# One long spectral piece to a tick in place of two, and the second run of gates four ticks later

## The chip, the cores and the metric

The kernel runs on one core of a Trainium2 chip. The metric is the device time of one execution in microseconds (us). Before the change the median of three runs is 10126.7 us (10123.93 to 10132.92).

## The reference: what is computed

The input `x` is 8 elements of 8 channels of 512 x 512 numbers in fp32. Two layers follow each other, and both add their result to their input.

```python
x = x + _L0_conv_ref(_gn(x), ...)   # spectral layer
x = x + _L1_conv_ref(_gn(x), ...)   # cellular automata and a gate
```

Layer 0 normalises in groups, takes every second row and column, keeps 8 x 4 modes of the two-dimensional Fourier transform, mixes the channels of each mode with complex weights, and evaluates the result at all 512 x 512 points. Layer 1 normalises the sum again. It runs 15 steps of a coupled map, with a hidden network and a gate beside it:

```python
for _ in range(STEPS):
    mapped = R * grid * (1.0 - grid)
    local = _conv(mapped, K_local, groups=C_OUT)
    physics = (1.0 - EPS) * mapped + EPS * local
    grid = (1.0 - BETA) * physics + BETA * drive
cml_out = jnp.clip(grid, 0.0001, 1.0 - 0.0001)
h = jax.nn.relu(_conv(x, Wp, bp))
nca_out = jax.nn.sigmoid(_conv(h, Wu, bu))
gin = jnp.concatenate([x, cml_out, nca_out], axis=1)
g = jax.nn.sigmoid(_conv(jax.nn.relu(_conv(gin, Wg1, bg1)), Wg2, bg2))
return g * cml_out + (1.0 - g) * nca_out
```

## The kernel before

The program is written out in full, in one order per engine, which `keep_order` fixes: every engine executes its instructions in the order of the source. There is no loop on the device. Dependences between engines are semaphores, and all loads and stores of the main part are issued by SyncE (SP) in order.

The eight elements go through a pipeline. While element b runs the coupled map and the hidden network, the gates of element b-1 are computed and the spectral layer of element b+1. Time is planned in ticks, 75 (`TICKS`) to an element. One call of `work` emits one tick:

- Two convolutions of the coupled map (`convolve`, L523), one per set of 128 partitions; 192 matmul records of L528 in a tick. The map's channels are two halves of four, each half five sets and fifteen steps. `settle` (L577) adds the drive `dE` or `dO` on VectorE (L583) and squares on ScalarE (L589); at step 13 `dO` is shifted on GpSimd (L593). `renew` (L535) exchanges the edges of the sets by small DMAs.
- None, one or two rounds of the hidden network (`Hidden.round`, L620): 24 matmul records each (L628), evicted half by ScalarE (L634) and half by VectorE (L636). After each second round, `Hidden.point` (L643) multiplies `h` by `w_u` (L647).
- Other work, handed out by `Others`. `Others.first` comes between the rounds and `Hidden.point` and gets two pairs of PSUM banks; `Others.second` comes after it and gets one. `first` takes a gate's 3 x 3 convolution (`Gate.conv`, L693) if one was loaded in an earlier tick, and then `second` takes its pointwise part (`Gate.point`, L710). Without a gate both take pieces of the spectral layer.

The spectral layer of an element, `layer0` (L318), is a generator cut into pieces by `yield`. Before each piece stands what it needs (`need`): a channel number means that this channel must have been fetched in an earlier tick; `LATER` (-2) that the piece may only be the first of its call; `LONG` (-1) or a channel number makes it a long piece; nothing means that it may come at any time. In order the pieces are: eight transforms, one per channel (four bn_stats on VectorE, L332; matmuls L336); the statistics (`group_stats`, L299, matmuls L303 and L311); the mixing of modes (L361 to L391); and then for each channel the first half of the synthesis (L430, an addition L433 and two bn_stats L435), the rows of the next channel (`over_rows`, L395, matmuls L398, evicted by ScalarE L402), and the second half, with the statistics and the normalising (L414) of each pair of channels in between. `Element.spectral` (L771) refuses a long piece when the tick has already had two, counted in `Others.longs`.

`Others.feed` (L793) runs at the start of a tick. It loads gates, up to two waiting at a time, in ticks from `GATES[0]` on and before `GATES[1]`, and again from `GATES[2]` on; an element has 43. A gate's load is six DMAs, three into `gin` and three into `mix`, in slots of a pool of five (`shared`) that the fetched channels of `x` use too. From tick 26 (`SPECTRAL_FROM`) on it fetches up to two channels of `x` per tick, 1 MB each and sixteen in all, when a slot is free. After `feed`, `Half.prepare` (L495) loads `dE` and `dO` of the next half into 15 slots (`sets`) as they come free; for the next element this begins in tick 70. It also emits the scaling of `dO` (L521) on GpSimd and the first square (L508) on ScalarE.

On GpSimd a gate has a subtraction (L703) and a product (L721); VectorE closes it with L726 in the next tick, between the two settlings, and SP stores it (L733).

As the code orders it, a middle element (1 to 6) has in ticks 3 to 27 the first 25 gates, in 28 to 45 the spectral pieces, in 46 to 51 nothing besides the map and the hidden network, in 52 to 69 the other 18 gates, and in 70 to 74 nothing again. Element 0 has no gates, and its spectral pieces stand in ticks 0 to 18. Element 7 has gates and no spectral pieces. After it a tail computes the last element's hidden rounds and gates.

Of the kernel before, what the change touches and what calls it, by code (L numbers as in the profile page):

```python
# [52 lines left out]
GR = 12  # L53
TICKS = STEPS * 5
ROUNDS, ROUNDS_LAST, FIRST_ROUNDS = 128, 48, 8
GATES, SPECTRAL_FROM = (2, 27, 51), 26
SLAB, HALO, SETS = 32, 3, 5
SHARED = 5
LONG, LATER = -1, -2
# [67 lines left out]
def conv_layers(ctx: ExitStack, tc: tile.TileContext, a, out):  # L127
# [614 lines left out]
    class Element:  # L742
# [28 lines left out]
        def spectral(self, ps, n, longs):  # L771

            need = self.need
            if not self.pieces or need == LATER and n or need is not None and need >= LONG and longs > 1:
                return False
            if need is not None and need >= 0 and now[0] <= self.at.get(need, now[0]):
                return False
            self.bank.append(ps)
            self.need = next(self.pieces, self)
            self.bank.clear()  # L780
            if self.need is self:
                self.pieces, self.need = None, None
            return True
# [216 lines left out]
```

## Time and profile before

| | us |
|---|---|
| median of the runs | 10126.7 |
| profiled execution, its own time | 10129.58 |
| its span | 10127.8 |
| VectorE busy | 5848.6 |
| ScalarE busy | 4299.5 |
| GpSimd busy | 1766.8 |
| mean granted clock of TensorE (share) | 0.983 |

The profile is that of one execution. Lines are those of the kernel; busy is the time in which an engine had an instruction running; an arrow in a row points to what ended a wait. "issue" stands for time in which an engine waited for nothing that the profile shows. TensorE's weight loads (PEld) overlap its matmuls. The granted clock is the share of full speed that TensorE's throttle allowed; a DMA share is the mean busy share of the 16 DMA engines.

### The profile page before, as it was taken

The page shows a single profiled execution, that of the slowest core. Times are in us where ns is not written, and L with a number is a line of the kernel's source. Part 1 is how long each engine was busy: PE and PEld are TensorE (multiplying, and loading weights), DVE is VectorE, ACT ScalarE, POOL GpSimd, SP SyncE. Part 2 cuts the span into 40 slices and gives each one's busy share as a digit, 9 for nine tenths or more (in the row PEclk, how much of TensorE's full clock was granted, in tenths as well). Part 3 has the DMA queues.
Part 4 walks back from the last instruction along what each step waited for, and adds up shares of the span by engine and source line. Part 5 has one row for each costly group of instructions (what it writes and reads, how often), then busy time and mean ns, then how long its engine had stood idle before and what let it go on. Part 6 is the DMA issues. An engine that isn't in the chain of part 4 may idle for free. (4 is left out here: it accounts for less than half of the span.)

```text
span 10127.8 us, 353307 instructions
## 1 busy us (share of the span) xinstructions
PE 9436.5 (93%) x160496; PEld 4308.9 (43%) x160496; DVE 5848.6 (58%) x6067; ACT 4299.5 (42%) x4445; POOL 1766.8 (17%) x1406
## 2 busy tenths in 40 slices
PE   6998999999999999999999999999999999998999
PEld 3444444444444444444444444444444444444333
DVE  5654555755557555665555655566555665555555
ACT  2444444444444444444444444444444444444433
POOL 2010111202112021111211112111121201312212
PEclk9999999999999999999999999999999999999999
DMA  5231255535555465544555455554555535663578
GB/s 170 81 84 48 62 147 137 152 103 141 142 149 147 109 150 135 153 138 121 142 137 147 127 123 144 138 141 129 134 146 134 157 117 132 155 145 95 139 194 199
DMA packets 625565, 1353.50 MB, mean 134 GB/s; under 512 B 73067, under 2 KB 73195, under 8 KB 594051
## 3 DMA queue, kind: packets, MB, share of 16 engines
q1 hardware_dynamic: 621728, 1329.77, 50.7%
q8 instruction: 1261, 20.66, 0.9%
q14 instruction: 238, 1.94, 0.1%
q10 hardware_dynamic: 2338, 1.13, 0.0%
HBM read 992.27 MB, written 268.78 MB: 125 GB/s over the span
## 5 line engine op out<-in xcount | busy, mean ns | idle before, releaser
L528 PE MATMUL pair<-m,band 32*32 32x512 f32 x115200 | 4118.2, 608 | 177.2 <-issue 109.1
L589 ACT ACTIVATE m<-m 128x1024 f32<-128x1024 f32 x2240 | 2360.0, 1055 | 2811.5 <-DVE m L583 2695.1
L528 PEld LDWEIGHTS pair<-m,band 32*32 32x32 f32 x115200 | 2268.6, 104 | 1943.4 <-issue 1106.4
L628 PE MATMUL pair<-cols,w_p 32*128 32x511 f32 (+1 forms) x24576 | 2874.7, 605 | 42.8 <-issue 22.2
L583 DVE SCALAR_TENSOR_TENSOR m<-pair,dO 128x1024 f32<-128x1024 f32 x1280 | 1507.5, 1219 | 1372.5 <-PE pair L528 1176.3
L583 DVE SCALAR_TENSOR_TENSOR m<-pair,dE 128x1024 f32<-128x1024 f32 x1120 | 1319.7, 1220 | 1222.4 <-PE pair L528 1039.2
L628 PEld LDWEIGHTS pair<-cols,w_p 32*128 32x128 f32 x24576 | 1284.6, 187 | 1647.0 <-issue 1138.0
L636 DVE TENSOR_SCALAR h<-pair,b_p 128x1024 f32<-128x1024 f32 x1024 | 1313.5, 1283 | 838.7 <-PE pair L628 838.2
L634 ACT ACTIVATE h<-pair,b_p 128x1024 f32<-128x1024 f32 x1024 | 1140.7, 1114 | 990.0 <-PE pair L628 981.7
L721 POOL TENSOR_TENSOR mix<-mix 96x512 f32<-96x512 f32 x344 | 437.5, 1272 | 4413.2 <-ACT mix L719 4067.7
L647 PE MATMUL pair<-h,w_u 128*32 128x512 f32 x8192 | 1014.9, 606 | 205.4 <-DVE h L636 189.3
L698 PE MATMUL pair<-gin,w_g 128*32 128x511 f32 (+1 forms) x8256 | 965.7, 599 | 5.9 <-DMA mix<-xn 3.3
L703 POOL TENSOR_TENSOR mix<-mix 96x512 f32<-96x512 f32 x344 | 437.9, 1273 | 1420.7 <-DMA mix<-nca 1340.7
L593 POOL TENSOR_SCALAR dO<-dO 128x2048 f32<-128x2048 f32 x80 | 431.7, 5408 | 1263.2 <-DVE m L583 1263.1
L647 PEld LDWEIGHTS pair<-h,w_u 128*32 128x32 f32 x8192 | 254.3, 110 | 848.8 <-issue 367.6
L660 ACT ACTIVATE y<-y,b_u 128x512 f32<-128x512 f32 x256 | 184.8, 722 | 908.4 <-DVE y L656 908.4
L698 PEld LDWEIGHTS pair<-gin,w_g 128*32 128x32 f32 x8256 | 237.2, 110 | 681.6 <-issue 464.8
L715 PE MATMUL pair<-mix,w_g 128*32 128x512 f32 x2064 | 358.8, 595 | 85.2 <-DVE mix L708 85.2
L654 ACT COPY y<-pair 128x512 f32<-128x512 f32 x256 | 149.9, 585 | 631.1 <-PE pair L647 527.0
L708 DVE TENSOR_SCALAR mix<-pair,b_g 128x512 f32<-128x512 f32 x344 | 257.9, 750 | 254.2 <-PE pair L698 254.2
L726 DVE SCALAR_TENSOR_TENSOR mix<-mix,back 96x512 f32<-96x512 f32 x344 | 316.1, 919 | 150.8 <-POOL mix L721 150.8
L521 POOL TENSOR_SCALAR dO<-dO,base 128x512 f32<-128x512 f32 x320 | 226.8, 724 | 783.0 <-DMA dO<-xn 728.0
(85 smaller groups left out, 2642.2 us busy)
## 6 DMA issues: line engine op xcount, KB each, us to landing
gin<-xn SPq DMA_DIRECT2D x344, 384.0 KB
cols<-xn SPq DMA_DIRECT2D x256, 512.0 KB
x<-in_x SPq DMA_DIRECT2D x120, 1024.0 KB
gin<-cml SPq DMA_DIRECT2D x344, 320.0 KB
gin<-nca SPq DMA_DIRECT2D x344, 320.0 KB
dE<-xn SPq DMA_DIRECT2D x320, 256.0 KB
dO<-xn SPq DMA_DIRECT2D x320, 256.0 KB
mix<-xn SPq DMA_DIRECT2D x344, 192.0 KB
```

What stands on the lines that cost most here:

```text
L528: nc.tensor.matmul(ps[h // 2][32 * t : 32 * t + 32, h % 2], band[at, c0 + (t if step % 2 else h), dx], m[at, t, dx : dx + N], start=(n == ...
L583: nc.vector.scalar_tensor_tensor(u[:, at], ps[q], FLOOR, d[:, at], ALU.max, ALU.add)
L589: nc.scalar.square(u[:, at], u[:, at])
L593: nc.gpsimd.tensor_scalar(d, d, 0.5, None, ALU.add)
L628: nc.tensor.matmul(ps[g // 2][:, g % 2, lo:hi], w_p[p, dx, i % 2], self.cols[p, i // 2, at : at + hi - lo], start=(n == 0), stop=(n == 2), ...
L634: nc.scalar.activation(h[:, :2], ps[0], AF.Relu, bias=b_p)
L636: nc.vector.tensor_scalar(h[:, 2:], ps[1], b_p, 0.0, ALU.add, ALU.max)
L647: nc.tensor.matmul(ps[32 * g : 32 * g + 32], w_u[:, r % 4], h[:, g], start=(r == self.hs[0][0]), stop=(r == self.hs[-1][0]), tile_position ...
L698: nc.tensor.matmul(ps[32 * j : 32 * j + 32, lo:hi], gband[:, dx], gin[:, j, at : at + hi - lo], start=(n == 0), stop=(n == 2), tile_positi ...
L703: nc.gpsimd.tensor_tensor(d, d, ng, ALU.subtract)
L715: nc.tensor.matmul(ps[at], gpoint[:, at], mix[:, 3], start=True, stop=True, tile_position=(0, 32 * j),)
L721: nc.gpsimd.tensor_tensor(d, d, mix[: GR * C, 2], ALU.mult)
```

## The change

Two numbers. In `Element.spectral`, a long piece is refused when the tick has had one long piece already, in place of two. `GATES[2]`, the tick from which an element's second run of gates is loaded, is 55 in place of 51.

```diff
@@ -53,7 +53,7 @@
 GR = 12
 TICKS = STEPS * 5
 ROUNDS, ROUNDS_LAST, FIRST_ROUNDS = 128, 48, 8
-GATES, SPECTRAL_FROM = (2, 27, 51), 26
+GATES, SPECTRAL_FROM = (2, 27, 55), 26
 SLAB, HALO, SETS = 32, 3, 5
 SHARED = 5
 LONG, LATER = -1, -2
@@ -771,7 +771,7 @@
         def spectral(self, ps, n, longs):
 
             need = self.need
-            if not self.pieces or need == LATER and n or need is not None and need >= LONG and longs > 1:
+            if not self.pieces or need == LATER and n or need is not None and need >= LONG and longs:
                 return False
             if need is not None and need >= 0 and now[0] <= self.at.get(need, now[0]):
                 return False
```

With it the spectral pieces of a middle element stand in ticks 28 to 54, tick 55 has neither pieces nor gates, the 18 gates of the second run stand in 56 to 73, and tick 74 has nothing again. In element 0 the pieces stand in ticks 0 to 27. No instruction is added or removed, and the tail's order is the same.

## The prediction

> **What bounds the kernel now.** I read the page first. TensorE is busy 93% of the span, VectorE 58%, ScalarE 42%: TensorE is the bound, and what can be won is in its gaps.
>
> ```profile
> PE 9436.5 (93%) x160496; PEld 4308.9 (43%) x160496; DVE 5848.6 (58%) x6067; ACT 4299.5 (42%) x4445; POOL 1766.8 (17%) x1406
> q8 instruction: 1261, 20.66, 0.9%
> ```
>
> The table of waits, filtered to PE (total us, times, longest), names the gaps. The reader is to see three kinds: waiting for the hidden layer's eviction, waiting for statistics, and "issue", in which nothing in the trace is waited for.
>
> ```profile
> PE pair L647 <- DVE h L636: 189.3, 147, 1.6
> ...
> PE pair L528 <- issue: 109.1, 65, 4.5
> ...
> PE pair L303 <- DVE mv L294: 79.2, 26, 12.5
> ```
>
> Then the timeline of PE. A tick begins with 192 records of L528, so counting 192 of them divides the trace into 600 ticks, 75 for an element. Tick numbers below count from an element's start; means are over elements 1 to 6, whose plans are alike. First an empty tick (element 2, tick 50): 1.52 us pass before L647, since only then is h there.
>
> ```profile
> 3363.02 6.58 PE L528 MATMUL pair<-m,band 32*32 32x512 f32 x192
> 3369.53 5.43 PE L628 MATMUL pair<-cols,w_p 32*128 32x512 f32 x48
> 3376.48 1.92 PE L647 MATMUL pair<-h,w_u 128*32 128x512 f32 x16 [1.52 <-DVE h L636]
> ```
>
> Then tick 44, where two synthesis halves (both L430, a "long" piece each) stand in one tick and the statistics at once need them. The eight L430 take 1.04 us; VectorE's additions and bn_stats for both make PE wait 3.37 us.
>
> ```profile
> 3285.79 1.04 PE L430 MATMUL pair<-e,ty 8*128 8x512 f32 x8
> 3287.40 1.92 PE L647 MATMUL pair<-h,w_u 128*32 128x512 f32 x16 [0.57 <-DVE h L636]
> 3292.70 0.58 PE L303 MATMUL pair<-mv,avg 128*128 128x1 f32 x2 [3.37 <-DVE mv L294]
> ```
>
> Last the windows, one per tick (span, then busy time of PE, PEld, DVE, ACT, POOL, granted clock, DMA share, GB/s): ticks 35, 41, 50, 51, 52 and 70 to 74 of element 2. In the spectral ticks 35 and 41 the clock falls to 0.79 and 0.90; an empty tick is 15.31, a gate tick 17.21; 51, with two gate loads at once, 20.31; DMA is idle in 70, 0.72 busy in 71 and 72, full in 73 and 74.
>
> ```profile
> 3122.68:3140.48 17.80, 17.41 (x244) 7.62 (x245) 14.21 (x15) 1.51 (x2) 7.64 (x9) 0.79 1.03 243
> 3224.60:3240.73 16.13, 15.72 (x251) 7.10 (x249) 11.58 (x12) 6.40 (x7) 0.00 (x0) 0.90 0.60 210
> 3363.02:3378.33 15.31, 13.79 (x260) 6.67 (x256) 7.97 (x7) 7.07 (x7) 0.00 (x0) 1.00 0.33 78
> 3378.33:3398.64 20.31, 16.01 (x260) 6.79 (x256) 7.28 (x6) 6.93 (x7) 1.26 (x1) 0.92 0.65 155
> 3398.64:3415.85 17.21, 17.21 (x290) 7.73 (x286) 9.38 (x9) 7.65 (x8) 0.00 (x0) 1.00 0.41 111
> 3698.78:3714.09 15.31, 13.79 (x259) 6.70 (x256) 7.94 (x7) 7.03 (x7) 1.98 (x2) 1.00 0.16 51
> 3714.09:3729.41 15.32, 13.80 (x260) 6.66 (x257) 7.97 (x7) 7.06 (x7) 0.31 (x1) 1.00 0.72 166
> 3729.41:3744.73 15.32, 13.79 (x261) 6.65 (x257) 8.42 (x7) 4.93 (x5) 2.40 (x4) 1.00 0.72 172
> 3744.73:3761.16 16.43, 14.22 (x260) 6.36 (x257) 10.33 (x9) 2.95 (x3) 3.41 (x7) 1.00 0.96 239
> 3761.16:3776.75 15.59, 14.11 (x260) 7.15 (x256) 9.55 (x8) 6.61 (x5) 3.80 (x9) 1.00 0.97 256
> ```
>
> Over ticks 28 to 74 a middle element takes 777.2 us: 41.4 of waits, 10.4 of "issue", 35.3 at half clock. Waits and issue off, and half of the half-clock time, 707.8 remain as TensorE's work, which the change doesn't touch.
>
> [...] eight L430 take 1.04 us, four 1.03. [...] The page's q8 line is that (20.66 MB in 1261 packets, 16.4 KB each); not hidden here: I take "issue" to be PE waiting for such a block behind bursts of data.
>
> **The change, part by part.** No instruction is added; only the order differs. [...] Empty ticks outside 0 to 2 fall from 11 (46 to 51, 70 to 74) to two (55, 74). The number of hidden rounds in a tick (two, or one in pairs of ticks) keeps its place.
>
> *Spectral ticks.* A two-round tick holds 13.80 us of work and 1.52 of wait. A transform piece adds 0.96 (two make 15.71, no wait left, so (15.71 - 13.80)/2), a synthesis half 0.93 (the wait falls from 1.52 to 0.59 with one): alone each fits into the wait, and the tick stays at about 15.35.
> - 28 to 35, the eight transforms: 12.5 (one round) + 5 x 15.4 + 10.9 + 14.3 = 114.7. In 35 the wait for statistics stays in part: four bn_stats (2.4 us) fewer lie before it, but also one transform on PE; 1.4 in place of 3.3.
> - 36 to 38, means and mixing, as now: 17.6 + 15.5 + 17.6 = 50.7.
> - 39 to 52, synthesis: seven two-round ticks with one half each, 15.35 to 15.6, together 108.2; 43, 44 and 51 (over_rows with a half, 2.1 of work against 1.5 of wait, like today's 16.40 in tick 43) 16.8, 16.3, 16.4; one-round ticks 40, 41, 47, 48, estimated between an empty 10.7 or 11.9 and today's 14.5 to 17.3 with two halves: 12.8, 12.2, 15.0, 14.2. Together 211.9.
> - 53: as 44 now (19.18) less one addition and two bn_stats (1.20 + 1.29): 16.7. 54: 10.9.
> - Dips: from 27 us of half clock in ticks 28 to 45 I leave 12, a loss of 6. Bounds: 0 and 13.5, all of today's loss.
> - The fetches of x spread from ticks 27 to 33 over 27 to 36 and meet the loads of the second half (tick 35 is at 1.03): 3 for issue, between 0 and 6. On SP such a fetch waits for the slot's last bn_stats (L332; SP waits 68.2 us for it in all, 10 times); behind it stand dE loads that are issued two ticks ahead: nothing.
>
> Together 413.9 for 28 to 54, with 55 at 16.5: 11.9 empty plus 4.6, since today's tick 51 is 5.2 over empty in the mean for the same double load, and moves with it.
>
> *Gates.* 56 to 69 are gates before and after: 241.0. 70 to 73 turn from empty (61.9) into two-round gate ticks of 17.7, today's mean, 70.8. 74: 16.2.
>
> *What collides.* Gate loads now issue in ticks 70 to 72, each six DMAs of 1.6 MB ahead of the next element's dE and dO on SP's queue; the out store, waiting for L726 on SP, joins up to 74. A gate tick's DMA share is near 0.6, an empty one's 0.16, so a load is 0.45 x 17 = 7.6 us of all engines, three 23 us. The slack in 70 to 72 is (0.84 + 0.28 + 0.28) x 15.3 = 21 us, plus 6 from longer ticks. It just fits, in bursts of 3.6 MB in 71 and 72, larger than tick 51's 3.2. I take 8 us of issue and dips; the bounds are 1 and 23 (the rival below). On POOL, the dO scaling (L521, 2.7 us, waiting for its load) now stands ahead of L703 and L721 in 72 and 73. Behind L721 waits L726 on VectorE, ahead of the next settling. I put the load that it waits for 10 to 16 us later in 73 than now; with 2.7 + 1.3 + 1.3 L721 ends between 15 and 21 us after that tick's start, and L726 is due at 17.2 + 5: nothing, with 1 us of cover.
>
> Sum per middle element: 413.9 + 16.5 + 241.0 + 70.8 + 16.2 + 8 = 766.4, against 777.2: -10.8. The same by gaps: 707.8 + 29 of waits + 16 of issue + 8.5 of dips = 761.3, -15.9. I take -13, times six -78. Element 0 has no gates: 27 ticks (1 to 27) of 424.5 us hold 34.2 of waits and 47.8 at half clock; spread out I make them 403, -21. Element 7's gates only change places with empty ticks; the tail is the same: 0. Total -99. The profiled execution took 10129.58 for a span of 10127.8; the median is 10126.7, 3 us lower. 10126.7 - 99 gives 10028.
>
> **Rivals.**
> 1. *Dips go and the collision is harmless*: the sum without the allowances of 6, 3 and 8 is 749.4, with 1 for the collision 750.4, -26.8 per element, and -21 for element 0: 9945. For it: gate ticks elsewhere lose only 0.5 us to bursts, and 73 and 74, full of DMA, hardly any. [...]
> 2. *Dips stay as they are*[...]. 7.5 us more per element (13.5 in place of 6) leaves -5.5, with the collision at 12 in place of 8 it leaves -1.5; element 0 keeps half, -10: 10084 to 10108. I take 10100, where faster and no change meet. [...]
> 3. *Slower: the next element's loads come late.* In element 7, ticks 36 to 39, loads of a half meet short ticks; those four take 57.8 us where their likes take about 35, 23 lost.
>
> ```profile
> 9192.69 4.52 PE L528 MATMUL pair<-m,band 32*32 32x512 f32 x128 [3.29 <-issue]
> ...
> 9207.95 3.98 PE L628 MATMUL pair<-cols,w_p 32*128 32x512 f32 x17 [4.13 <-issue]
> ```
>
> The place is ticks 71 to 77: gate loads stand ahead of dE and dO in SP's order and on the DMA engines. It decides once the last dO lands over 9 us later than now: its scaling (L521) ends at 3795.2 in element 2, and the settling that adds it stands in tick 77, which begins at 3800.9 and convolves for 3 us first. Price: 23 at the boundary as in element 7, in place of the 8, and if the three gate loads stay almost wholly unhidden (20 late of 23) another 20 - 9 = 11 in the first ticks; 26 x 6 = 156 over the forecast: 10184. Against: 27 us of slack for 23 of loads.
>
> That the change doesn't do what it says can be excluded: the order of pieces follows from the code alone.
>
> **How the numbers follow.** Forecast 10028: 0.47. Rival 1: 0.20. Rival 2: 0.18, of it 0.08 within no change. Rival 3: 0.15. A measurement here tells 0.2%, 20 us, from none. Faster 0.77, same 0.08, slower 0.15. The range, 9930 to 10140, leaves out rival 3 and a quarter of rival 1.
>
> **What would show it.** L647's wait for h falls well below 189 us; L303's wait falls from 79 to about 50; tick 53 is near 16.7; the clock in the spectral ticks is above 0.95. Wrong, if issue grows by over 10 us per element in ticks 70 to 77, if L528 or L508 waits there for dE, or if the half-clock time stays at 338 us.

## The result, and the profile after

The change made the kernel slightly faster: median 10093.04 us of six runs (10081.33 to 10109.42) against 10125.32 us before (six runs), ratio 0.9973 with a 95% interval of 0.9961 to 0.9985. That is 32 us, a third of the 99 that were forecast. The profiled execution of the changed kernel is the fastest of its six, so the two profiles lie 48.7 us apart (spans 10079.1 and 10127.8), more than the medians. Where parts are added up below, they are parts of these 48.7.

The first lines are from the page of the changed kernel and from its table of waits, filtered to PE (total us, times, longest). The last line is L398's in the kernel before.

```profile
PE 9432.0 (94%) x160496; PEld 4303.4 (43%) x160496; DVE 5851.5 (58%) x6067; ACT 4294.7 (43%) x4445; POOL 1768.5 (18%) x1406
...
PE pair L647 <- DVE h L636: 130.5, 150, 1.6
PE pair L528 <- issue: 125.0, 73, 4.4
...
PE pair L528 <- ACT h L634: 50.5, 40, 11.5
PE pair L303 <- DVE mv L294: 47.3, 19, 12.4
PE pair L398 <- ACT h L634: 39.5, 27, 8.7
```

```profile
PE pair L398 <- ACT h L634: 10.5, 15, 0.9
```

The reader is to see two falls and two rises. The waits that the change aims at fell as forecast: L647's for `h` from 189.3 to 130.5 us, L303's for statistics from 79.2 to 47.3. But L398 now waits 39.5 us for ScalarE (before: 10.5, and never over 0.9), and L528's issue went from 109.1 to 125.0.

The timeline of PE shows that the pieces alone behave as worked out. Tick 53 of element 2 has one half of the synthesis before the statistics, and the wait, 3.37 us in tick 44 before, is now 0.93:

```profile
3368.90 1.02 PE L430 MATMUL pair<-e,ty 8*128 8x512 f32 x4
3370.50 1.92 PE L647 MATMUL pair<-h,w_u 128*32 128x512 f32 x16 [0.57 <-DVE h L636]
3373.36 0.38 PE L303 MATMUL pair<-mv,avg 128*128 128x1 f32 x2 [0.93 <-DVE mv L294]
```

The loss is in the windows of ticks 36 to 38 of element 2 (span, busy time of PE, PEld, DVE, ACT, POOL, granted clock, DMA share, GB/s), below with ticks 70 to 74. The last line is tick 38 of the same element in the kernel before, where synthesis pieces stand in it:

```profile
3074.05:3092.13 18.08, 17.01 (x323) 8.78 (x323) 12.38 (x23) 7.92 (x8) 4.90 (x6) 1.00 0.99 265
3092.13:3114.82 22.69, 17.40 (x259) 6.92 (x257) 10.39 (x12) 8.36 (x7) 7.93 (x11) 0.85 0.95 234
3114.82:3142.29 27.47, 20.19 (x276) 7.69 (x273) 12.52 (x18) 10.98 (x10) 10.83 (x10) 0.79 0.48 122
...
3643.01:3660.16 17.15, 17.15 (x289) 7.66 (x287) 10.04 (x10) 7.03 (x7) 3.23 (x3) 1.00 0.59 146
3660.16:3678.40 18.24, 18.24 (x289) 7.74 (x286) 9.34 (x9) 8.23 (x9) 2.51 (x2) 1.00 0.95 187
3678.40:3695.55 17.15, 17.15 (x290) 7.59 (x287) 12.12 (x11) 5.03 (x5) 5.70 (x6) 1.00 0.63 141
3695.55:3717.66 22.11, 19.66 (x289) 7.81 (x286) 12.54 (x11) 4.11 (x5) 5.22 (x6) 0.92 1.02 231
3717.66:3734.03 16.37, 14.89 (x260) 7.12 (x257) 10.38 (x9) 6.81 (x5) 5.11 (x9) 1.00 0.95 244
```

```profile
3176.51:3193.89 17.38, 17.38 (x274) 9.64 (x272) 13.47 (x14) 11.74 (x11) 10.84 (x10) 1.00 0.89 321
```

Tick 38 takes 27.47 us with TensorE's clock at 0.79. Of the gate ticks at the end, which I had feared, only 73 is much longer than a gate tick elsewhere (21.2 us in the mean of the six elements).

Split into ticks as in the prediction, a middle element (mean of 1 to 6, us) came out so:

| ticks | forecast | after |
|---|---|---|
| 28 to 35, transforms | 114.7 | 117.8 |
| 36 to 38, means and mixing | 50.7 | 66.2 |
| 39 to 52, synthesis | 211.9 | 213.6 |
| 53, 54 | 27.6 | 27.2 |
| allowances for dips and fetches, held in the rows above | 9 | |
| 55 | 16.5 | 13.2 |
| 56 to 69 | 241.0 | 240.2 |
| 70 to 74 | 95.0 | 91.2 |
| 28 to 74 | 766.4 | 769.4 |

Before, 28 to 74 took 777.2. Ticks 0 to 27 became 3.1 longer, so a middle element gains 4.8 (1241.7 to 1236.9), of a forecast of 13. Element 0 gained 26.4, element 7 lost 7.3.

What happens in tick 38 stands in four timelines of the changed kernel, of SP, GpSimd, ScalarE and PE in this order:

```profile
3115.14 0.38 SPq L611 DMA_DIRECT2D cols<-xn  x1
3117.77 0.79 SPq L391 DMA_DIRECT2D om<-of_sin  x1
3118.61 3.42 SPq L569 DMA_DIRECT2D cml<-m  x4
```

```profile
3127.99 0.11 POOL L507 MEMSET m<- 128x8 f32 x1 [17.20 <-DMA cml<-m]
```

```profile
3116.30 1.99 ACT L508 ACTIVATE m<-dE,mhalf 128x2048 f32<-128x2048 f32 x1
3128.14 2.00 ACT L508 ACTIVATE m<-dE,mhalf 128x2048 f32<-128x2048 f32 x1 [9.85 <-POOL m L507]
3130.04 2.93 ACT L589 ACTIVATE m<-m 128x1024 f32<-128x1024 f32 x3
3132.88 1.09 ACT L634 ACTIVATE h<-pair,b_p 128x1024 f32<-128x1024 f32 x1
```

```profile
3121.97 5.48 PE L628 MATMUL pair<-cols,w_p 32*128 32x512 f32 x48
3134.03 1.93 PE L398 MATMUL pair<-e,om 16*32 16x512 f32 x8 [6.57 <-ACT h L634]
```

Read from below: PE's L398 waits 6.57 us for ScalarE's L634. L634 stands in ScalarE's order behind L508, the square of the fifth set of the second half, which waits 9.85 us for GpSimd's memset L507. The memset waits for the slot that the last set of the first half leaves, that is for its store `cml<-m`. SP issued this store at 3118.61, behind `om<-of_sin`, the store of the mixing's result. L398 waits in this way in tick 38 of all six middle elements, 1.3 to 8.7 us each.

In the kernel before, the same store went out before its tick 38 began at 3176.51. The memset waited there for VectorE and not for the store, and ScalarE waited 1.19 us for it (SP, GpSimd and ScalarE):

```profile
3172.61 3.82 SPq L569 DMA_DIRECT2D cml<-m  x4
```

```profile
3181.68 0.11 POOL L507 MEMSET m<- 128x8 f32 x1 [12.18 <-DVE m L583]
```

```profile
3181.82 2.00 ACT L508 ACTIVATE m<-dE,mhalf 128x2048 f32<-128x2048 f32 x1 [1.19 <-POOL m L507]
```

The mixing lay in ticks 32 and 33, and `om<-of_sin` went out at 3108.32, just after tick 34 began. SP stood waiting for VectorE there too, and longer: 126.4 us in the whole kernel before, 67.4 in the changed one. But in element 2 the next `cml` store came 25 us behind it. What changed is not the wait, but what stands behind it.

### The profile page after: what moved, and what is told of

The parts are those of the page before. It is cut to its first block, busy times and chain, and to the rows that moved or that the text cites. A ratio compares the mean times of both kernels' runs of the same rounds, so it can differ in the third digit from the quotient of the medians.

```text
span 10079.1 us, 353020 instructions
## 1 busy us (share of the span) xinstructions
PE 9432.0 (94%) x160496; PEld 4303.4 (43%) x160496; DVE 5851.5 (58%) x6067; ACT 4294.7 (43%) x4445; POOL 1768.5 (18%) x1406
## 3 DMA queue, kind: packets, MB, share of 16 engines
q8 instruction: 1261, 20.66, 0.9%
## 5 line engine op out<-in xcount | busy, mean ns | idle before, releaser
L528 PE MATMUL pair<-m,band 32*32 32x512 f32 x115200 | 4107.0, 605 | 205.4 <-issue 125.0
L528 PEld LDWEIGHTS pair<-m,band 32*32 32x32 f32 x115200 | 2256.1, 103 | 1945.9 <-issue 1111.4
L634 ACT ACTIVATE h<-pair,b_p 128x1024 f32<-128x1024 f32 x1024 | 1140.3, 1114 | 995.7 <-PE pair L628 977.7
L647 PE MATMUL pair<-h,w_u 128*32 128x512 f32 x8192 | 1010.1, 604 | 153.0 <-DVE h L636 130.5
L647 PEld LDWEIGHTS pair<-h,w_u 128*32 128x32 f32 x8192 | 250.9, 110 | 787.1 <-issue 383.8
```

What stands on the lines that cost most here:

```text
L528: nc.tensor.matmul(ps[h // 2][32 * t : 32 * t + 32, h % 2], band[at, c0 + (t if step % 2 else h), dx], m[at, t, dx : dx + N], start=(n == ...
L634: nc.scalar.activation(h[:, :2], ps[0], AF.Relu, bias=b_p)
L647: nc.tensor.matmul(ps[32 * g : 32 * g + 32], w_u[:, r % 4], h[:, g], start=(r == self.hs[0][0]), stop=(r == self.hs[-1][0]), tile_position ...
```

## The experiments

Theory A: the early part of the spectral layer, one transform to a tick, ate the gain, since it moves fetches and mixing onto the half boundary in ticks 35 to 38. Its variants are A1, the fetches of `x` collide with the second half's loads; A2, the mixing's store stands before the cml store in SP's order; A3, the moved pieces keep the engines busy there. Theory B: the gates' shift ate it. Theory C: splitting the synthesis gains little. All ratios are against the kernel before on the same chip, with its 95% interval; before ran in 10127.46 us beside the first four runs and in 10125.95 beside the others.

**The gates alone** (`e1_gates_only`).

```diff
-GATES, SPECTRAL_FROM = (2, 27, 51), 26
+GATES, SPECTRAL_FROM = (2, 27, 55), 26
```

> Two long pieces to a tick as before, only the second run of gates four ticks later. Theory A (the early transforms, one to a tick, ate the gain; the gates' shift costs little): per middle element +12 for ticks 70 to 73, -10 for 52 to 55, +3 in the next element's first ticks, and +7 in element 7: +35 in all, 10145 to 10170 beside about 10125 before. Theory B (the gates' shift ate it): +70 or more, 10195 and up. If the shift costs nothing: 10125.

Measured: 10161.32 us, ratio 1.0036 (1.0021 to 1.005). That is about 34 us more: the shift costs what A puts on it, not what B needs. In its profile ticks 70 to 74 take 94.0 against 78.1, 51 to 55 take 68.6 against 83.4, and the next element's ticks 0 to 2 take 2.7 more. By itself the shift is a loss. It is the price of having ticks 51 to 54 for the spectral layer.

**The synthesis alone** (`e3_late_one_51`): two transforms to a tick as before, of the later long pieces one.

```diff
-need is not None and need >= LONG and longs > 1:
+need is not None and need >= LONG and longs > (0 <= need < C):
```

> Two transforms to a tick as before, one synthesis piece to a tick as in the change, gates at 51 as before (the pieces just fit, ticks 28 to 50). Theory A: ticks 34 to 50 fall from 274 to about 255 in each middle element, element 0 gains 15: -100 to -130, 9995 to 10025. Theory C (splitting the synthesis gains only what fills empty ticks, 5 to 8 us per element): -30 to -60, 10065 to 10095. Theory B expects the same as A here, since the gates stay.

Measured: 10066.83, ratio 0.9939 (0.9924 to 0.9954), a gain of 61, just above the upper end of C's range and well below A's. So one part of the change, without the gates' shift that it doesn't need, gives about twice the whole change. Ticks 34 to 50 take 269.3 us in its profile (273.9 before), where A expected 255. In them ticks 35 to 38 still take 72.5 us (73.9 before), with 4.8 of issue and 10.1 at half clock: the half boundary has stalls with synthesis pieces in it too.

**The transforms alone** (`e4_early_one`).

```diff
-need is not None and need >= LONG and longs > 1:
+need is not None and need >= LONG and longs > (not 0 <= need < C):
```

> One transform to a tick as in the change, two synthesis pieces as before, gates at 51. Theory A: ticks 28 to 38 cost 184 as in the changed kernel, later ones as before: +10 per middle element, -10 in element 0: +30 to +60, 10155 to 10185. Theory B: a gain of 5 to 10 per element from transforms that fit into the wait for h: -40 to -60, about 10075.

Measured: 10144.55, ratio 1.002 (1.0012 to 1.0029): slower, by less than A expected, and not the gain of B. Ticks 28 to 34 fall to 99.5 us from 115.4, and 35 to 38 rise to 83.8, tick 38 alone to 26.3, nearly the changed kernel's 84.3 and 26.4. The loss there, against the forecast, comes with the transforms' order and without the gates' shift. Against before, it is another place that makes this variant slower: ticks 28 to 38 together are 6.0 us shorter (183.3), and 39 to 54 are 10.4 longer (264.6), since the synthesis pieces that stood in 34 to 38 now follow there, two to a tick.

**Fetches held back** (`e5_hold_x`): of the sixteen fetches of `x`, the last seven wait until tick 38. It is the changed kernel with

```diff
-                if spectral and (t >= SPECTRAL_FROM or not e):
+                if spectral and (t >= SPECTRAL_FROM or not e) and (not e or after.fetched <= C or t >= 38):
```

> The changed kernel, but the second copies of x after the first wait until tick 38, so that four fetches leave ticks 33 to 36. Theory A1 (these fetches meet the loads of the second half): ticks 35 to 38 fall from 84 to 68 to 72, -70 to -100 against the changed kernel's 10093, 9995 to 10025. Theory A2 (not the bytes, but the pieces of the mixing and their stores in SP's order at the half boundary): within 15 of 10093. Theory B: within 15 of 10093.

Measured: 10089.03, ratio 0.996 (0.9945 to 0.9974), like the changed kernel. A1 as the only cause falls. Issue in tick 37 went from 2.5 to 0.1 us, but tick 38 stayed at 25.7. SP's timeline says why:

```profile
3108.39 0.38 SPq L611 DMA_DIRECT2D cols<-xn  x1
3114.65 0.79 SPq L391 DMA_DIRECT2D om<-of_sin  x1
3115.49 3.00 SPq L569 DMA_DIRECT2D cml<-m  x4
```

SP has issued all that stood ahead by now, and stands still from 3108.8 to 3114.65, until VectorE has finished the mixing. The store behind it goes out no earlier in the tick than in the changed kernel (3.8 us after its beginning).

**The store of om behind the cml store** (`e6_om_later`): `later(1, ...)` puts it at the end of its tick. It is the changed kernel with

```diff
-        nc.sync.dma_start(out=om[8:, :, :8], in_=of_sin)
+        later(1, lambda: nc.sync.dma_start(out=om[8:, :, :8], in_=of_sin))
```

> The changed kernel, but the store of of_sin into om is issued at the end of its tick, behind the store of the last set of the first half in SP's order. Theory A2 (in tick 37 this store waits on SP for VectorE's mixing, the cml store behind it is late, the memset of the fifth square waits for that slot, ScalarE waits for the memset, and L398 waits for ScalarE): tick 38's wait of 5.4 us and its dips shrink, 26.4 becomes 18 to 20, -40 to -50 against the changed kernel's 10093: 10043 to 10055. Theory A1 (bytes alone make these loads late): within 15 of 10093. Theory A3 (the pieces themselves keep the engines busy at the half boundary): within 15 of 10093.

Measured: 10094.78, ratio 0.9959 (0.9944 to 0.9974). A2 as the only cause falls as well. In two of the six middle elements the cml store now goes out 2.7 to 2.8 us before tick 38; in the others it goes out between 0.5 us before and 4 us after the tick's beginning, with SP still behind with loads. By the profile these wait for fetches of `x` to land, 2.0 to 4.8 us in each of the six from tick 36 on. Tick 38 takes 24.4.

**Both** (`e7_om_later_hold_x`): the two edits above together.

> As before it, and the second copies of x after the first wait until tick 38. If both lateness of SP and bytes hold up the same slot, neither alone frees it, and together they bring ticks 35 to 38 from 84 to 70 to 73: -60 to -80 against 10093, 10015 to 10035. If the order on SP is all: as the run before it. Theory A3: within 15 of 10093.

Measured: 10035.75, ratio 0.9901 (0.9884 to 0.9917), a gain of 90 over before and 57 over the changed kernel, with intervals that don't touch (the changed kernel's is 0.9961 to 0.9985). The cml store goes out 2.5 to 2.8 us before tick 38 in all six elements. Its timelines of SP, GpSimd and PE in element 2, whose tick 38 begins at 3117.84:

```profile
3115.04 3.02 SPq L569 DMA_DIRECT2D cml<-m  x4
...
3120.81 0.79 SPq L391 DMA_DIRECT2D om<-of_sin  x1
```

```profile
3123.43 0.11 POOL L507 MEMSET m<- 128x8 f32 x1 [11.51 <-DMA cml<-m]
```

```profile
3124.35 5.48 PE L628 MATMUL pair<-cols,w_p 32*128 32x512 f32 x48
3129.76 1.06 PE L398 MATMUL pair<-e,om 16*32 16x512 f32 x8
```

The memset comes 5.6 us after the tick's beginning in place of 13.2, and L398 no longer waits. Tick 38 is 18.7 in the mean in place of 26.4, and ticks 35 to 38 are 74.4 in place of 84.3. That is 9.9 for each of six elements, so the whole gain over the changed kernel lies there. So two delays of the same store lie on top of each other: the fetches of `x` and a waiting DMA, both ahead of it on SP. Each hides the other, and only without both the slot comes free in time. Whether the fetches hold SP up by their bytes or by their turns in its order these runs don't separate. A3, which expected a time within 15 us of the changed kernel's, can't be the main cause; ticks 35 to 38 stay 9.4 us above the 65.0 of the forecast's rows, and for that it isn't ruled out.

In ticks 28 to 54, 9.4 us fall away with both edits (424.8 to 415.4): 3.2 of waits, 3.2 of issue, and 5.7 at half clock, which is an estimated 2.9 of loss (half of it: in element 2 of the changed kernel the sixteen L647 of tick 38 ran at a clock of 0.50 and took 3.64 us, those of tick 53 at 1.00 and took 1.92). The fetches alone (`e5_hold_x`) took 3.7 of issue away there, but 1.3 more of waits and 3.4 more at half clock took a part of that back.

**One gate load to a tick** (`e8_one_load`): the synthesis-alone kernel, and in `feed`

```diff
                 g.load()
                 self.loaded.append(g)
+                if t < TICKS:
+                    break
```

> Two transforms and one synthesis piece to a tick with gates at 51, as the run of that name, and at most one gate load to a tick, so that ticks 2 and 51 have one load of 1.6 MB in place of two. If the issue stalls there come of the double load: -5 in tick 51 and -2 in tick 2 of each middle element, -30 to -45 against that run's 10067: 10022 to 10037. If they come of any load: within 10 of 10067.

Measured: 10046.09, ratio 0.9913 (0.9895 to 0.9931). It is 21 us below the synthesis alone, but the intervals overlap, so whether the double load's burst causes the issue stalls is not settled. In the profile issue in ticks 51 to 55 falls from 1.6 to 0.8 us and in 0 to 2 from 1.9 to 1.2, less than expected.

**All three** (`e9_all`): the changed kernel with the fetches held, the store later and one load to a tick.

> The changed kernel with all three: the store of om later, the copies of x held back, one gate load to a tick. The sum of what each theory gives: A2 with A1 -60 to -80 and the single load -30 to -45, 9970 to 10005; theory A3 with the single load alone: 10050 to 10065.

Measured: 10025.4, ratio 0.9892 (0.9875 to 0.991), 20 above the range for the sum. It has the lowest median of all and is faster than the kernel before and the changed one, but it isn't told apart from the two edits without the single load.

## Why the prediction was right or wrong

- *Direction, and what TensorE waited for*: right. The pieces fit into the wait for `h`; two-round ticks with one transform take 15.2 us (forecast 15.4), tick 53 takes 16.6 (16.7), ticks 39 to 54 together 240.8 (239.5).
- *"36 to 38, means and mixing, as now: 17.6 + 15.5 + 17.6"*: this is the step that failed. The pieces are the same, but their place isn't: they moved from ticks 32 to 34 onto the half boundary. There they took 66.2 us in place of 50.7, 15.5 more for each of six elements, 93 in all, and tick 35 took 18.1 in place of 14.3. The prediction followed a fetch of `x` on SP, found dE loads behind it, and put that at nothing; in the changed kernel SP's loads of dE and dO wait 55.3 us for such fetches, which they didn't before. And it did not list the two DMAs of the mixing, and so missed that `om<-of_sin` waits for VectorE with the first half's last store behind it. With both delays taken out, 36 to 38 take 55.7; the 5.0 left over 50.7 have no experiment of their own.
- *How the miss adds up*: 13 us were forecast for a middle element and 4.8 measured. Ticks 28 to 54 are 10.9 over their sum (the 9 of allowances are in it), tick 55 is 3.3 under, 56 to 74 are 4.6 under, and 0 to 27, put at nothing, are 3.1 over. The other 2.2 come of taking -13 where the sum by parts said -10.8. With element 7 and element 0 below, that makes the 50 us between the 99 forecast and the 48.7 of the two profiles.
- *"3 for issue, between 0 and 6"* for the fetches: held as far as issue goes. Without them tick 37 falls from 19.9 to 17.1. What they also do is keep SP late, so that moving the other store alone doesn't help. That the prediction didn't have.
- *Dips, 12 us of half clock left*: too few. In ticks 28 to 54 25.6 remain of 30.7 before, 16.4 of them in 35 to 38, where the stalls are. In ticks 28 to 34 they went from 5.8 to nothing.
- *The collision in 70 to 74*: 95.0 forecast, 91.2 measured, so the allowance of 8 was about 4 too large. Rival 3's mechanism exists in small: in four of the six middle elements tick 1 has 3.6 to 4.9 us of waits in place of 1.6, and in element 7 L528 waits 11.5 us in one stroke. That is the chain of tick 38 again, at the boundary between two elements: ScalarE's L508 waits 12.17 us for the memset L507, and GpSimd waits 12.65 us for a load ahead of the memset and 5.09 for a `cml` store. Element 7, put at nothing, lost 7.3. The slower case as a whole didn't come.
- *Element 0*: -21 forecast, -26.4 measured. The 5.4 more are luck: they hide a part of the loss.
- *Rival 2*, dips unchanged, came nearest with its 10100, and partly for its reason: it put the loss to dips at 13.5 us per element, and half of the 25.6 above, by the same estimate, is 12.8. But with both delays taken out 19.9 remain of the 25.6, so a part of these dips went away with the late slot, and the late slot, with its 57 us, was in no rival.

With both delays taken out, ticks 28 to 54 take 415.4 us (413.9 forecast) and the kernel 10035.75 (10028). So near the forecast the sum comes partly because its errors offset each other: more time at half clock than allowed, less in tick 55 and in 70 to 74, more gained in element 0. The moved mixing, with what stands around it on SP, was the error that mattered.

## What to carry to other kernels

A piece that moves takes its DMAs with it, and on an in-order queue it is the instructions behind it in the new place that pay (here 57 us came back when two delays ahead of one store on SP were taken out): list each DMA, what it waits for, and whose slot the next one frees. Work that fits into a gap on one engine should be placed where other queues are idle too; here the boundary between two halves has little to spare (a DMA share of 0.99 and 0.95 in ticks 36 and 37). When an edit that should remove a delay shows nothing, a second delay may hide it: try both at once before the theory is dropped.

## What the runs showed of the hardware

In tick 38 of element 2 a stall of 6.57 us stood beside a clock of 0.79 over that tick. In the mean of the six elements the tick has 5.4 us of waits and 9.6 at half clock (a clock of 0.50 in the records), against 0.8 and 2.4 once the slot was free in time (`e7_om_later_hold_x`). So 4.6 us more of waits went with 7.2 us more at half clock, which by the estimate above (half of it) is another 3.6 us lost. Half is the upper end: in the kernel before, the matmuls of L647 came 213 ns apart at half clock and 107 at full, but those of L528 44 and 35 (medians). What brings the clock down isn't shown.

The prediction took "issue" for TensorE waiting for a late block of instructions, and the DMA records of the ten traces fit that. After the first 150 us, they have 863 such gaps of TensorE of 0.3 us or more, and every one ends 1.2 to 1.8 us after a packet of the instruction queue (q8, 1261 packets with a mean of 16.4 KB in the kernel before) has ended; of moments picked at random 13% have the end of such a packet 1 to 2 us before them. That TensorE waits for these packets is an estimate from this. What would make them late isn't shown.

Before's time ranged from 10099.13 to 10155.57 us in 32 runs, so that a difference of a few tenths of a per cent needs several runs of each.
